# A four-layer convolution chain on one core: storing the Haar coefficients so that a step of the mixing stage reads one contiguous run of DRAM

## The chip, the core and the metric

The kernel runs on one core of a Trainium2 chip. The metric is the device time of one execution in microseconds. Before the change it is 2869.11 us, the median of 7 runs (2862.92 to 2873.05).

## The reference

The input x has shape (4, 64, 256, 256): images, channels, rows, columns, in float32. Four layers follow each other.

```python
x = conv(x, L0)      # per channel: a causal 2-D convolution with an outer-product filter, plus x * bias
x = haar_layer(x)    # L1
x = conv(x, L2)
x = conv(x, L3)

def haar_layer(x):
    f1 = haar2d(x)
    acc = 0
    for i in range(2):
        f4 = einsum('bchw,oc->bohw', f1 * v[i], conv_w[i])
        acc += sign(f4) * relu(abs(f4) - tau[i])
    return haar2d(acc, inverse=True) + x
```

The filters of the convolution layers come from small sine networks. Since the filter of a channel is an outer product, the convolution is a multiplication by one triangular Toeplitz matrix along the rows and another along the columns. The convolutions and the Haar transforms act on one channel at a time; the mixing in L1 acts on all 64 channels at one position. That is why the data changes its order twice, through DRAM.

## The kernel before

The four images are two groups of two. Three phases work on each group.

- **Phase A** (`phase_a`, L422) goes through a group in 32 rounds of two channels. A round loads x (L136, 1 MB), multiplies by the Toeplitz matrices `tx` and `ty` (L149, six DMAs of 64 KB), does the forward Haar transform along one axis on POOL (L355, L357) and along the other on PE (L319), and stores its 1 MB of coefficients in the DRAM tile `coef` of the group (`store`, L481 to L483).
- **Phase B** (`phase_b`, L524) goes through a group in 64 steps. A step takes a 1/64 part of the coefficients of all 64 channels. `load` (L539) fetches it in two DMAs (`ft<-coef`, L545), and also `v` and `tau` for the step (L551, 512 KB each). Per step there are two units: PE mixes the channels (L590), DVE multiplies by v (L605), ACT takes sign and magnitude (L609, L613), DVE subtracts tau and thresholds (L616, L619), POOL adds up (L631 to L635). `store` (L638 to L640) writes the result to the DRAM tile `mixed` in two DMAs.
- **Phase C** (`phase_c`, L687) goes through a group in 32 rounds again: `load` (L694 to L699) fetches a round's 1 MB from `mixed` into the tile `g`, the inverse Haar transform follows, then the two convolutions L2 and L3 (L307), and the output is stored (L766, L762).

The work is laid side by side by a function `beside` (L817), which mixes the pieces of two phases in program order. First comes phase A of group 0 alone, then phase A of group 1 beside phase B of group 0, then a short changeover, then phase C of group 0 beside phase B of group 1, then phase C of group 1 alone. The order on every engine's queue is that order of the program. All DMAs are issued by SP, one after the other, from one queue; a DMA that must wait holds up every DMA behind it.

A DRAM tile for coefficients (`coefficients`, L103) has the shape [2, 32, PAIR]: 64 blocks, each of PAIR elements (L77). Before the change PAIR is 133,120 elements, that is 520 KB. Two functions say which bytes a DMA touches:

- `all_rows` (L415), used by L483 and L699, gives the rows of one round. SBUF partition p = 2m + q belongs to block m. For each q there is one DMA of 64 rows: 8 KB at an offset of (32 q + r) x 8 KB in block m, for round r. So the 64 rows of a DMA lie at a pitch of 520 KB.
- `step_of` (L532), used by L545 and L640, gives the rows of one step. For each channel parity e there is one DMA of 64 rows of 4 KB. They all lie in block 32 e + s // 2, at a pitch of 8 KB; an even step s takes the first half of each 8 KB, an odd step the second half.

Of the kernel before, what the change touches and what calls it, by code (L numbers as in the profile page):

```python
# [47 lines left out]
P = 128  # L48
# [17 lines left out]
NB = B // GROUPS  # L66
CI = 4 // NB
M = CI * NB

ROUNDS = C // CI  # L70
STEPS = C
# [2 lines left out]
C_PIECES = 4 * BLOCKS + 2  # L74
W = 2 * N

PAIR = 2 * ROUNDS * 2 * NB * W + 2 * NB * W  # L77


IMAGES = (GROUPS, NB, ROUNDS, CI, BLOCKS, ROW, N)  # L80
# [11 lines left out]
def conv_haar_kernel(  # L92
# [10 lines left out]
    def coefficients(name):  # L103
        return dram.tile([CI, STEPS // 2, PAIR], F32, tag=name, name=name)

# [308 lines left out]

    def all_rows(grp_tile, r, images):  # L415

        by_q = images.rearrange("(m q) n k -> q m (n k)", q=2)
        n = 2 * NB * W
        at = [grp_tile.offset + (q * ROUNDS + r) * n for q in range(2)]
        return [(bass.AP(grp_tile.tensor, at[q], [[PAIR, P // 2], [1, n]]), by_q[q]) for q in range(2)]  # L420

    def phase_a():  # L422

# [57 lines left out]
        def store(t):  # L481
            for to, f in all_rows(coef[t // ROUNDS], t % ROUNDS, st[t]["f"]):
                nc.sync.dma_start(to, f)  # L483
            st[t].clear()
# [39 lines left out]
    def phase_b(grp):  # L524
# [7 lines left out]
        def step_of(ap, s, images):  # L532

            n = NB * W
            by_e = images.rearrange("(m e) b w -> e m (b w)", e=CI)
            at = [ap.offset + (e * STEPS // 2 + s // 2) * PAIR + s % 2 * n for e in range(CI)]
            return [(bass.AP(ap.tensor, at[e], [[2 * n, P // CI], [1, n]]), by_e[e]) for e in range(CI)]

        def load(s):  # L539
            if s >= STEPS:  # L540
                return
            d = st[s]
            d["f"] = bp.tile([P, NB, W], F32, tag="ft", name=f"ft_{grp}_{s}", bufs=4)
            for rows, f in step_of(coef[grp], s, d["f"]):
                nc.sync.dma_start(f, rows)  # L545
            for name, src in (("v", v), ("tau", taus)):
                t = d[name] = bp.tile([P, 2, W], F32, tag=name, name=f"{name}_{grp}_{s}", bufs=3)

                at = src.offset + s * 4 * W * COPIES
                flat = bass.AP(src.tensor, at, [[2 * W, 2 * COPIES], [0, C // COPIES], [1, 2 * W]])  # L550
                nc.sync.dma_start(t.rearrange("p e w -> p (e w)"), flat)  # L551
# [86 lines left out]
        def store(s):  # L638
            for to, g in step_of(mixed[grp], s, st[s]["g"]):
                nc.sync.dma_start(to, g)  # L640
            st[s].clear()
# [45 lines left out]
    def phase_c():  # L687
# [6 lines left out]
        def load(t):  # L694
            if t >= total:
                return
            st[t]["g"] = big("in", f"g_{t}", 3)
            for rows, g in all_rows(mixed[t // ROUNDS], t % ROUNDS, st[t]["g"]):
                nc.sync.dma_start(g, rows)  # L699
# [263 lines left out]
```

## Time and profile before

| What | Value |
|---|---|
| Median of 7 runs | 2869.11 us |
| The profiled execution itself | 2869.66 us |
| Its span, first to last instruction | 2867.9 us |
| Mean granted TensorE clock | 0.934 |
| PE / PEld busy share | 85% / 68% |
| DVE / ACT / POOL busy share | 55% / 50% / 68% |
| DMA bytes, mean rate | 636.27 MB, 222 GB/s |
| DMAs issued by SP for coef, g | 128 and 128, 512 KB each |
| DMAs issued by SP for ft, mixed | 256 and 256, 256 KB each |

The profile is of one execution. Busy time is that of an engine in all; it says little about what limits a stage, since the stages differ. The times of the stages in this execution, from the first and last issue of their DMAs: the first ft is issued at 452.4 us, the last coef of group 1 at 1264.9 us, the last mixed of group 1 at 2156.9 us. A line such as "ft<-coef SPq ... x256, 256.0 KB, 8.4" gives a kind of DMA, the number of issues, the size of one and the median time from its issue to its landing. The chain of waits is followed back from the last instruction, at each step to what released it.

### The profile page before, as it was taken

What the parts mean: (1) busy time and instruction counts of PE and PEld (TensorE: products, weight loads), DVE (VectorE), ACT (ScalarE), POOL (GpSimd) and SP (SyncE); (2) the same over time, 40 slices, a digit from 0 to 9 for tenths busy, and PEclk for the clock granted to TensorE, in tenths of its full rate; (3) what the DMA queues carried; (4) which work ended last, traced back from release to release, by engine and by line L of the source; (5) the groups of instructions that cost most, each with busy time, mean ns of one, the idle gap of its engine ahead of it and who ended that gap; (6) DMA issues with size and microseconds to landing.
All of it is one profiled execution on the core that took longest, in us unless ns stands there. A gap on an engine that the chain in (4) does not pass through costs nothing.

```text
span 2867.9 us, 119602 instructions
## 1 busy us (share of the span) xinstructions
PE 2437.6 (85%) x53276; PEld 1948.4 (68%) x53276; DVE 1582.9 (55%) x1779; ACT 1428.4 (50%) x2361; POOL 1950.5 (68%) x2422
## 2 busy tenths in 40 slices
PE   6999998677767667759888888898898999999999
PEld 5777776454445444537777666676677888888888
DVE  2453335677777767536777766766772333333333
ACT  1222224566566666527676666676673333333332
POOL 2777876877778777748878767777775555555551
PEclk9999998788888887979999999999999999999999
DMA  5668777799898999766888888888885444444432
GB/s 156 230 211 252 249 270 237 239 274 284 284 286 274 271 282 272 243 194 205 251 266 233 260 249 246 246 261 243 249 253 172 147 141 152 138 157 132 161 114 93
DMA packets 223290, 636.27 MB, mean 222 GB/s; under 512 B 39078, under 2 KB 121671, under 8 KB 190264
## 3 DMA queue, kind: packets, MB, share of 16 engines
q1 hardware_dynamic: 222776, 628.62, 70.5%
q8 instruction: 419, 6.86, 1.0%
q14 instruction: 95, 0.78, 0.1%
HBM read 413.12 MB, written 215.35 MB: 219 GB/s over the span
## 4 chain that ended last, share of the span: by engine, by line
PE 40%; DMA 23%; DVE 8%; POOL 5%; issue 4%; ACT 4%; SPq 3%; DVEq 0%; ACTq 0%; POOLq 0%
PE c1c L307 9%; PE c2r L307 8%; DMA ft<-coef 8%; PE c2c L307 7%; PE c1r L307 6%; DMA v<-in_v 5%; PE c0ps L319 3%; PE f L590 3%; DMA mixed<-gt 2%; DMA tau<-taus 2%; DMA g<-mixed 2%; DVE a L616 2%; DVE x L605 2%; DMA tx<-filt 1%; PE a1ps L307 1%
## 5 line engine op out<-in xcount | busy, mean ns | idle before, releaser
L392 POOL TENSOR_TENSOR i<-i,g 128x16 f32<-128x16 f32 x744 | 394.8, 551 | 477.7 <-ACT g L375 458.7
L590 PE MATMUL f<-ft,mix 64*64 64x512 f32 x2048 | 345.3, 686 | 248.3 <-DMA ft<-coef 173.0
L605 DVE TENSOR_TENSOR x<-f,v 128x1024 f32<-128x1024 f32 x256 | 312.1, 1219 | 261.1 <-PE f L590 129.1
L307 PEld LDWEIGHTS a1ps<-tx,x 64*64 64x64 f32 x8192 | 324.8, 142 | 111.3 <-issue 51.9
L609 ACT ACTIVATE m<-x 128x1024 f32<-128x1024 f32 x256 | 272.2, 1063 | 223.1 <-DVE x L605 165.5
L307 PEld LDWEIGHTS c1c<-ty,ch 64*64 64x64 f32 x8192 | 307.8, 134 | 107.7 <-ACT ch L740 58.3
L307 PE MATMUL a1ps<-tx,x 64*64 64x192 f32 (+3 forms) x8192 | 356.3, 315 | 27.5 <-issue 7.5
L307 PE MATMUL c1c<-ty,ch 64*64 64x256 f32 (+3 forms) x8192 | 341.9, 302 | 34.4 <-issue 24.0
L307 PEld LDWEIGHTS c2r<-tx,cy 64*64 64x64 f32 x8192 | 305.7, 135 | 96.2 <-ACT ch L740 55.5
L307 PEld LDWEIGHTS a2ps<-ty,ay 64*64 64x64 f32 x8192 | 315.8, 142 | 77.5 <-issue 52.4
L307 PE MATMUL a2ps<-ty,ay 64*64 64x256 f32 (+3 forms) x8192 | 346.5, 314 | 14.4 <-issue 10.2
L307 PE MATMUL c2r<-tx,cy 64*64 64x256 f32 (+3 forms) x8192 | 339.3, 303 | 19.8 <-issue 11.7
L616 DVE TENSOR_TENSOR a<-a,tau 128x1024 f32<-128x1024 f32 x256 | 313.8, 1226 | 65.8 <-ACT a L613 64.9
L613 ACT ACTIVATE a<-x 128x1024 f32<-128x1024 f32 x256 | 264.7, 1034 | 168.6 <-DVE m L619 168.4
L631 POOL TENSOR_TENSOR gt<-gt,m 128x1024 f32<-128x1024 f32 x128 | 303.2, 2369 | 58.3 <-DVE m L619 55.7
L307 PE MATMUL c2c<-ty,ch 64*64 64x128 f32 (+3 forms) x8192 | 323.8, 300 | 12.5 <-issue 12.4
L740 ACT COPY ch<-c1r 128x512 f32<-128x512 f32 x256 | 137.2, 588 | 391.5 <-PE c1r L307 391.2
L307 PE MATMUL c1r<-tx,z 64*64 64x64 f32 (+3 forms) x8192 | 325.9, 301 | 5.7 <-issue 5.7
L307 PEld LDWEIGHTS c2c<-ty,ch 64*64 64x64 f32 x8192 | 307.5, 135 | 33.4 <-issue 20.8
L307 PEld LDWEIGHTS c1r<-tx,z 64*64 64x64 f32 x8192 | 304.1, 135 | 36.1 <-issue 21.2
L466 DVE SCALAR_TENSOR_TENSOR x<-x,bias_sb,a2ps 128x512 f32<-128x512 f32 x256 | 179.5, 742 | 269.1 <-PE a2ps L307 247.4
L619 DVE SCALAR_TENSOR_TENSOR m<-a,m 128x1024 f32<-128x1024 f32 x256 | 313.0, 1223 | 22.0 <-DVE a L616 0.5
(71 smaller groups left out, 3200.3 us busy)
## 6 DMA issues: line engine op xcount, KB each, us to landing
coef<-f SPq DMA_DIRECT2D x128, 512.0 KB, 5.7
ft<-coef SPq DMA_DIRECT2D x256, 256.0 KB, 8.4
v<-in_v SPq DMA_DIRECT2D x128, 512.0 KB, 8.4
tau<-taus SPq DMA_DIRECT2D x128, 512.0 KB, 10.2
mixed<-gt SPq DMA_DIRECT2D x256, 256.0 KB, 8.4
g<-mixed SPq DMA_DIRECT2D x128, 512.0 KB, 7.9
x<-in_x SPq DMA_DIRECT2D x63, 1024.0 KB, 6.5
out<-o SPq DMA_DIRECT2D x63, 1024.0 KB, 5.1
```

The source lines that it names most:

```text
L307: nc.tensor.matmul(ps[r][half(c), j % 2, k * ROW :], data[half(r), c, k, bass.ts(j, ROW)], t(r, c)[:, : N - k * ROW], start=k == 0, stop=k ...
L319: nc.tensor.matmul(ps[r][half(c)].rearrange("p h k -> p (h k)"), matrix[half(r)], pairs(r, c).rearrange("p h k -> p (h k)"), start=True, s ...
L392: engine.tensor_tensor(to, s, d, op)
L466: nc.vector.scalar_tensor_tensor(to, old, bias_sb[:, c : c + 1], ps, ALU.mult, ALU.add)
L590: nc.tensor.matmul(un[u]["f4"][half(q), b, :], mixers[0][half(r), bass.ts(i, C)], st[s]["f"][half(r), b], start=True, stop=True, tile_posi ...
L605: nc.vector.tensor_tensor(un[u]["x"], un[u]["f4"], both(u, "v"), ALU.mult)
L609: nc.scalar.activation(un[u]["m"], un[u]["x"], AF.Sign)
L613: nc.scalar.activation(un[u]["a"], un[u]["x"], AF.Abs)
L616: nc.vector.tensor_tensor(un[u]["a"], un[u]["a"], both(u, "tau"), ALU.subtract)
L619: nc.vector.scalar_tensor_tensor(un[u]["m"], un[u]["a"], 0.0, un[u]["m"], ALU.max, ALU.mult)
L631: nc.gpsimd.tensor_tensor(st[s]["g"], st[s]["g"], m, ALU.add)
L740: later(lambda y=y, ps=ps: nc.scalar.copy(y, ps))
```

## The change

Only addresses change. A block keeps its 512 KB of data (2 values of q, 32 rounds, 2 halves, 4 KB each). Inside a block the half h of a row's 8 KB now comes first in the order of addresses, before q and the round. A round's rows are therefore cut into 4 KB pieces, and the rows of one step and one parity lie next to each other, 64 x 4 KB in one run of 256 KB. The padding behind a block shrinks from 8 KB to 4 KB, which makes the pitch 516 KB. `all_rows` returns four pairs of DRAM rows and SBUF rows instead of two, so the loops at L482 and L698 issue four DMAs of 256 KB per round instead of two of 512 KB. `step_of` still returns two.

```diff
-PAIR = 2 * ROUNDS * 2 * NB * W + 2 * NB * W
+PAIR = 2 * 2 * ROUNDS * NB * W + NB * W
...
     def all_rows(grp_tile, r, images):
 
-        by_q = images.rearrange("(m q) n k -> q m (n k)", q=2)
-        n = 2 * NB * W
-        at = [grp_tile.offset + (q * ROUNDS + r) * n for q in range(2)]
-        return [(bass.AP(grp_tile.tensor, at[q], [[PAIR, P // 2], [1, n]]), by_q[q]) for q in range(2)]
+        parts = images.rearrange("(m q) (h n) k -> h q m (n k)", q=2, h=2)
+        n = NB * W
+        pairs = []
+        for h in range(2):
+            for q in range(2):
+                at = grp_tile.offset + ((h * 2 + q) * ROUNDS + r) * n
+                pairs.append((bass.AP(grp_tile.tensor, at, [[PAIR, P // 2], [1, n]]), parts[h][q]))
+        return pairs
...
             n = NB * W
             by_e = images.rearrange("(m e) b w -> e m (b w)", e=CI)
-            at = [ap.offset + (e * STEPS // 2 + s // 2) * PAIR + s % 2 * n for e in range(CI)]
-            return [(bass.AP(ap.tensor, at[e], [[2 * n, P // CI], [1, n]]), by_e[e]) for e in range(CI)]
+            at = [ap.offset + (e * STEPS // 2 + s // 2) * PAIR + s % 2 * P // CI * n for e in range(CI)]
+            return [(bass.AP(ap.tensor, at[e], [[n, P // CI], [1, n]]), by_e[e]) for e in range(CI)]
```

## The prediction

> **What bounds the kernel now.** I read the page's forty slices first, then a table of stretches, then the chain of waits stage by stage, then the DMA issues, and last SP's own order of issue.
>
> ```profile
> PE   6999998677767667759888888898898999999999
> ...
> DMA  5668777799898999766888888888885444444432
> ```
>
> Read the two rows together. The front (to about 450 us) and the back (from about 2160 us) are full on PE and easy on DMA. Between 450 and 1200 us the DMA row stands at 8 and 9 while PE falls to 6 and 7. The stretches (us, then busy PE, PEld, DVE, ACT, POOL, then clock, DMA share, GB/s) say it in numbers:
>
> ```profile
> 200.00:300.00 100.00, 95.46 (x2242) 77.65 (x2235) 35.88 (x53) 27.25 (x49) 76.65 (x130) 0.98 0.80 249
> ...
> 600.00:750.00 150.00, 107.61 (x1768) 71.04 (x1768) 108.72 (x101) 95.22 (x130) 118.64 (x136) 0.85 0.92 283
> ...
> 1570.00:1720.00 150.00, 126.12 (x2697) 97.99 (x2699) 102.86 (x104) 94.37 (x153) 105.44 (x110) 0.98 0.85 247
> ...
> 2400.00:2640.00 240.00, 239.00 (x6266) 212.39 (x6261) 84.07 (x120) 91.05 (x201) 135.83 (x190) 1.00 0.44 145
> ```
>
> So there are four stages: A alone (PE 95%), A with B (DMA 0.92), C with B (both high), C alone (PE over 99%, DMA 0.44). The chain of waits, cut to 450-1200, 1270-2160 and 2160-2867 us, agrees:
>
> ```profile
> by line: DMA ft<-coef 20.1%; DMA v<-in_v 17.4%; DVE a L616 5.6%; DMA x<-in_x 4.6%; issue 4.4%; DVE x L605 4.2%; DVE m L619 3.4%; DVE x L466 3.3%; PE f L590 3.2%; DMA tx<-filt 3.2%; DMA tau<-taus 2.8%; DMA coef<-f 2.8%; DMA mixed<-gt 2.6%; A
> ...
> by line: PE c1c L307 9.8%; issue 8.6%; PE c2r L307 8.3%; DMA ft<-coef 7.9%; PE f L590 7.5%; DMA g<-mixed 6.5%; DMA mixed<-gt 5.7%; DMA tau<-taus 4.8%; PE c2c L307 4.8%; PE c1r L307 4.3%; PE c0ps L319 3.2%; SPq L149 2.7%; DVE o L759 2.3%; DV
> ...
> by line: PE c2r L307 23.7%; PE c1c L307 22.5%; PE c2c L307 21.6%; PE c1r L307 20.4%; PE c0ps L319 9.5%; issue 0.9%; DMA g<-mixed 0.7%; DVEq L958 0.2%; ACT ch L740 0.2%; ACTq L958 0.1%; ACT g L375 0.0%; DVE o L759 0.0%; ACTq L375 0.0%
> ```
>
> Adding the DMA entries: about 0.54 of the first stretch is transfer time on the chain, about 0.28 of the second (20.1 + 17.4 + 4.6 + 3.2 + 2.8 + 2.8 + 2.6, and 7.9 + 6.5 + 5.7 + 4.8 plus some smaller ones that the full chain gives), under 0.01 of the third. Those shares are my exchange rate from DMA time to kernel time. The transfers concerned are these (KB each, median us to landing):
>
> ```profile
> coef<-f SPq DMA_DIRECT2D x128, 512.0 KB, 5.7
> ft<-coef SPq DMA_DIRECT2D x256, 256.0 KB, 8.4
> ...
> mixed<-gt SPq DMA_DIRECT2D x256, 256.0 KB, 8.4
> g<-mixed SPq DMA_DIRECT2D x128, 512.0 KB, 7.9
> ```
>
> Last, SP's place on the chain. A piece of the chain in time order (start, us, what):
>
> ```profile
> 704.26 0.75 SPq L483
> 705.01 0.05 issue
> 705.06 0.02 SPq L545
> 705.08 0.03 issue
> 705.10 0.71 SPq L545
> 705.82 0.05 issue
> 705.87 9.46 DMA ft<-coef
> ```
>
> Here ft, which PE will need, is issued only after the coef stores of L483, because one in-order queue issues both. SP's timeline gives the price of an issue:
>
> ```profile
> 104.37 0.52 SPq L149 DMA_DIRECT2D ty<-filt  x1
> 105.73 1.14 SPq L483 DMA_DIRECT2D coef<-f  x2
> ```
>
> 1.14 us for two, so about 0.57 us each, and g, ft and mixed issues have medians near that.
>
> **What the Trainium skill says.** The page "DMA: Bandwidth & Descriptors", section "Latency and other measured facts", reports that rows at a pitch of large powers of two lose up to half the rate, that 4 KB of padding restores it, and that contiguous rows are fine too. The old pitch of 520 KB and the new one of 516 KB are both padded, and the 8 KB pitch of a step is not in its table. The trace shows the padded layout running well: data packets of 8 KB take 309 ns at the fast end and coef lands in 5.7 us. Its section "Why a DMA increments its semaphore by 16 and not by 1" derives the engine count from the slowest dimension; 64 rows use 16 engines before and after. The trace agrees: 38,567 four-byte completion packets for 2,413 DMAs, 16 each. Its section "Rules for kernel authors" wants few large transfers; here the trace has its own durations, which I use.
>
> **The change, part by part.** The order of issue on every engine stays; PE, DVE, ACT and POOL keep the same instructions. On SP only L483 and L699 change, from two DMAs of 64 rows x 8 KB to four of 64 rows x 4 KB. Bytes are equal.
>
> 1. *Packets of coef and g.* The trace's packets by size: 4 KB take 159 ns at the fast end (5th percentile), 225 in the mean; 8 KB take 309 and 364. Two for one costs 2 x 159 - 309 = 9 ns at best, 2 x 225 - 364 = 86 ns at worst. Each DMA is 4 rows per engine. Of the 128 coef DMAs, 54 fall in A with B: 216 rows per engine, 2 to 19 us of DMA time, times 0.54: 1 to 10. Of the 128 g DMAs, 58 fall in C with B: 232 rows, 2 to 20 us, times 0.28: 1 to 6. I take 3 us for both, near the low end, because coef already runs at the fast end. The 64 coef DMAs before 450 us and the 62 g DMAs after 2160 us are hidden under PE; without that cover they would cost as much again.
>
> 2. *256 more issues on SP.* At 0.57 plus 0.1 us between issues, 54 more between 450 and 1200 us are 36 us of SP time, 58 more in C with B 39 us. Most of it replaces waiting: SP stands waiting for earlier landings anyway (the waits of SP list 33.2 us of L149 for v, 28.0 for tau, and a dozen rows more in the first stage). Summing the chain's own pieces, L483 lies on it for 16.9 us and L699 for 2.9, so at most another 20 us, at least 0. Queued behind them on SP are mixed, ft, v and tau of the next step, and PE (L590) and DVE (L605) wait for those. This includes the three joints where a whole group must land before the next stage starts (448, 1265 and 2160 us), where two more issues stand in the open, about 1.2 us each. I take 8 us. In A alone the 58 more issues (39 us over 350) are hidden by PE at 95%; if A were not PE-bound they would show.
>
> 3. *The window of landings.* The trace's DMAs use eight landing semaphores in turn (100 to 105, 107, 108), and SP waits for the DMA eight issues back. With coef or g in the window, eight DMAs hold less than before, but still 2 MB (8 x 256 KB), some 7 us of work at 283 GB/s; I count 0, between minus 5 and plus 5 us, as the places of the waits shift by two.
>
> 4. *A step's rows become one run of 256 KB (ft, mixed).* The trace has no such 4 KB transfer. Nearest rows: x is contiguous, and yet it has one of the longest pieces of the chain in A with B (13.32 us, at 1124.68); v and tau come from contiguous 64 KB, each row read eight times, and land in 8.4 and 10.2 us. Bound from above: if all 512 packets per engine of ft and as many of mixed fell from 225 to 159 ns, 1024 x 66 ns = 68 us of DMA time per stage, 68 x (0.54 + 0.28) = 55 us gained. Bound from below: ft becomes as slow against today as tau stands against ft (10.2 to 8.4, a fifth): 45 ns on 225, 512 x 45 = 23 us of DMA time per stage, times 0.82: 19 us lost. I take 0: being contiguous shows no advantage in this trace, and both ends stay for the range.
>
> Sum: 3 + 8 = 11 us. On the profiled execution of 2869.66 us (span 2867.9, 1.8 outside it) that is 2880.7; the median of the runs is 0.55 lower, so I say 2880 us. Every wait stays in its place, and what is late next is ft after L483, as now.
>
> **Rivals.** *R1, contiguous rows are faster (the other side).* One mechanism: ft and mixed reach fewer memory channels at 4 KB of every 8 KB, and the new layout spreads them. Place: the two B stages. Price: half the bound, 27 us, less the 11 us of cost: 2854. It decides from the point where a fifth of the bound (11 of 55 us, 13 of the 66 ns a packet) is won. For it: ft is the largest entry of the chain. Against: the neighbours that are contiguous, x, v and tau, show no such advantage. *R2, contiguity hurts and SP shows fully.* 19 us from point 4, 20 from SP, 4 from the packets: 43, so 2912. For it: one queue issues everything and L483 stands right ahead of ft. Against: SP spends much of its time in waits. *R3, nothing shows:* SP's issues replace waits altogether and the packets cost 2: 2871; it is the low end of my own case.
>
> **How the numbers follow.** The measurement can tell about 0.2%, 5.7 us. My case, with its own range 2868 to 2896, gets 0.52, of which R3's corner and its surroundings within 0.2% are 0.17; R1 0.28 (2815 to 2866), of which 0.02 is within 0.2%; R2 0.20 (2896 to 2925). Faster 0.26, same 0.19, slower 0.55. Leaving a tenth or so off each end gives 2842 to 2904.
>
> **What would show it.** Right: SP has 256 issues each of coef and g; the DMA share between 600 and 750 us stays at 0.92 or above with the same GB/s; ft and mixed land in about 8.4 us; L483 on the chain nearly doubles; C alone is unchanged. R1: ft and mixed land clearly sooner, GB/s there rises above 283 and the wait of PE L590 for ft shrinks from 142.1 us. R2: ft lands later and the waits of L590 and L605 grow. Wrong altogether: a change in A alone or C alone of more than 5 us, where I count everything as hidden.

## The result

The changed kernel takes 2841.67 us (median of 13 runs, 2824.6 to 2852.46). The kernel before, run beside it, takes 2866.35 us (median of 34 runs, 2854.89 to 2885.23). The ratio is 0.9909, with a 95% interval of 0.989 to 0.9928: faster by 0.9%, about 26 us. The forecast was 2880 us, slower by 11 us; the direction was wrong, and the low end of the range of 2842 to 2904 us misses the median by a hair.

The profiled execution of the changed kernel took 2837.24 us, with a span of 2835.5 us. The stretches that were shown of the kernel before, now of the kernel after (us; busy PE, PEld, DVE, ACT, POOL; clock, DMA share, GB/s):

```profile
200.00:300.00 100.00, 95.71 (x2313) 79.89 (x2305) 34.46 (x50) 27.80 (x51) 81.04 (x142) 1.00 0.84 250
600.00:750.00 150.00, 105.44 (x1668) 67.49 (x1672) 108.87 (x103) 91.61 (x122) 111.66 (x120) 0.83 0.92 275
1570.00:1720.00 150.00, 131.96 (x2824) 102.70 (x2820) 106.71 (x108) 99.70 (x160) 109.77 (x113) 0.97 0.85 259
2400.00:2640.00 240.00, 239.23 (x6290) 212.40 (x6282) 82.65 (x118) 92.35 (x204) 134.63 (x192) 1.00 0.46 148
```

The DMA share is the same as before in the stretches of A beside B and C beside B. The rate rose from 247 to 259 GB/s in the third row and fell from 283 to 275 in the second, so short stretches don't tell the story. The DMA issues do show a change (KB each, median us to landing):

```profile
coef<-f SPq DMA_DIRECT2D x256, 256.0 KB, 4.8
ft<-coef SPq DMA_DIRECT2D x256, 256.0 KB, 6.5
...
mixed<-gt SPq DMA_DIRECT2D x256, 256.0 KB, 7.3
g<-mixed SPq DMA_DIRECT2D x256, 256.0 KB, 6.3
```

ft lands in 6.5 us where it took 8.4, mixed in 7.3 instead of 8.4. That looks like the proof of faster reads, but the first experiment below takes it away again. The chain between 450 and 1200 us in the kernel after:

```profile
by line: DMA v<-in_v 18.7%; DMA tau<-taus 13.3%; DMA ft<-coef 12.2%; DMA x<-in_x 7.9%; DVE x L610 5.3%; DVE a L621 4.9%; DMA mixed<-gt 3.8%; issue 3.4%; DVE m L624 3.3%; POOL f L357 3.0%; POOL fw L355 3.0%; DVE x L471 2.9%; PE f L595 2.5%; 
```

ft has gone from 20.1% to 12.2%, but v and tau together have grown by more, from 20.2% to 32.0%. The whole chain has 672 us of DMA before and 669 us after: what has changed is which of a step's loads lands last.

The four stages, cut at the first issue of ft, the last of coef and the last of mixed, are better places to look. Before: A alone 452.4, A beside B 812.5, C beside B 892.0, C alone 711.0 us. After: 446.1, 806.5, 878.6, 704.2. These are single executions, and the profiled run of a kernel lies up to 13 us from the kernel's median, so a stage's difference of 6 us is weak evidence by itself. The two middle stages of the kernel before (those of the kernel after stand with experiment 6):

```profile
452.40:1264.90 812.50, 576.60 (x9389) 383.65 (x9385) 557.43 (x555) 470.60 (x648) 614.74 (x712) 0.84 0.85 263
1264.90:2156.90 892.00, 764.12 (x16468) 617.79 (x16463) 615.88 (x633) 581.74 (x934) 652.41 (x668) 0.95 0.83 245
```

Below, *busy DMA time* is the summed time of the packets in the kernel's own DMA queue, divided by 16 engines, counted from the trace of a stage. The DMA share in the views also holds two small queues that fetch instructions, and is about 0.01 higher than busy DMA time over the length of the stage.

### The profile page after: what moved, and what is told of

Its sections match the earlier page's. It is cut to its first block, busy times and chain, and to the rows that moved or that the text cites. A ratio compares the mean times of both kernels' runs of the same rounds, so it can differ in the third digit from the quotient of the medians.

```text
span 2835.5 us, 120133 instructions
## 1 busy us (share of the span) xinstructions
PE 2434.7 (86%) x53276; PEld 1942.1 (68%) x53276; DVE 1583.4 (56%) x1779; ACT 1428.6 (50%) x2361; POOL 1951.8 (69%) x2422
## 4 chain that ended last, share of the span: by engine, by line
PE 38%; DMA 24%; DVE 10%; POOL 5%; ACT 4%; issue 4%; SPq 2%; DVEq 0%; ACTq 0%; POOLq 0%
PE c1c L307 9%; PE c2r L307 8%; DMA v<-in_v 7%; PE c2c L307 7%; PE c1r L307 6%; DMA ft<-coef 5%; DMA tau<-taus 5%; PE c0ps L319 3%; PE f L595 3%; DVE x L610 3%; DVE a L621 2%; DMA x<-in_x 2%; DVE m L624 2%; DMA mixed<-gt 1%; DMA g<-mixed 1%
## 5 line engine op out<-in xcount | busy, mean ns | idle before, releaser
L307 PE MATMUL a1ps<-tx,x 64*64 64x256 f32 (+3 forms) x8192 | 359.3, 317 | 24.1 <-ACT f L484 6.8
L307 PE MATMUL c1c<-ty,ch 64*64 64x128 f32 (+3 forms) x8192 | 339.2, 301 | 21.4 <-issue 11.0
L307 PE MATMUL c1r<-tx,z 64*64 64x128 f32 (+3 forms) x8192 | 329.3, 302 | 6.0 <-issue 6.0
L307 PE MATMUL c2c<-ty,ch 64*64 64x256 f32 (+3 forms) x8192 | 320.4, 297 | 6.4 <-issue 6.3
```

The source lines that it names most:

```text
L307: nc.tensor.matmul(ps[r][half(c), j % 2, k * ROW :], data[half(r), c, k, bass.ts(j, ROW)], t(r, c)[:, : N - k * ROW], start=k == 0, stop=k ...
```

## The experiments

Three theories were put up. *Layout*: the addresses of a step's rows give the gain. *Pieces*: issuing 256-KB instead of 512-KB DMAs for coef and g gives it. *Pitch*: 516 KB instead of 520 KB gives it. All ratios are against the kernel before on the same chip, with 95% intervals.

**1. The pieces alone.** The old addresses, but four DMAs:

```diff
-        by_q = images.rearrange("(m q) n k -> q m (n k)", q=2)
...
+        parts = images.rearrange("(m q) (h n) k -> h q m (n k)", q=2, h=2)
...
+                at = grp_tile.offset + ((q * ROUNDS + r) * 2 + h) * n
+                pairs.append((bass.AP(grp_tile.tensor, at, [[PAIR, P // 2], [1, n]]), parts[h][q]))
```

> The layout of before (8 KB per round and row at 520 KB, step rows 4 KB at a pitch of 8 KB), but a round's stores and loads issued as four DMAs of 64 rows x 4 KB, as in the change. Layout theory (contiguous step rows give the gain): 1.000 to 1.005 of before, because only the issues and the smaller packets are left. Pieces theory (256-KB DMAs land sooner, the window of eight landings turns faster): 0.991, the whole gain of the change. If both have a share, about 0.995.

Measured: 0.9989 (0.9975 to 1.0003). The 256 further issues and the smaller packets together cost nothing that shows, and they aren't the gain. Yet ft in this kernel:

```profile
ft<-coef SPq DMA_DIRECT2D x256, 256.0 KB, 6.1
...
mixed<-gt SPq DMA_DIRECT2D x256, 256.0 KB, 7.6
```

6.1 us for ft, even less than after the change, with none of its gain. So a shorter time to landing is no sign of a shorter kernel here. The likely reason, which no run separates: that time counts what is queued ahead, and with halved DMAs of coef and g a queue of the same number of DMAs holds fewer bytes.

**2. The addresses alone.** The layout of the change, with two DMAs per round, each of 64 rows x 2 pieces of 4 KB:

```diff
+            rows = [[PAIR, P // 2], [2 * ROUNDS * n, 2], [1, n]]
+            pairs.append((bass.AP(grp_tile.tensor, at, rows), parts[q]))
```

> The layout of the change (step rows contiguous, 516 KB pitch, packets of 4 KB), but a round's stores and loads issued as two DMAs of 64 rows x 2 pieces of 4 KB, 512 KB each, as many issues as before. Layout theory: 0.991 or a little below (SP saves 256 issues). Pieces theory: 1.000 to 1.003.

Measured: 0.9924 (0.9906 to 0.9942). The layout carries the gain. The difference of 0.0015 to the full change isn't resolved.

**3. The pitch alone.**

```diff
-PAIR = 2 * ROUNDS * 2 * NB * W + 2 * NB * W
+PAIR = 2 * ROUNDS * 2 * NB * W + NB * W
```

> The kernel before with one constant changed: the padding behind a block is 4 KB instead of 8 KB, so the pitch of a round's rows is 516 KB instead of 520 KB. Layout theory and pieces theory: 1.000. Pitch theory (516 KB spreads a round's rows better than 520 KB, and the rest of the change costs nothing): 0.991.

Measured: 0.9998 (0.9982 to 1.0014). The pitch theory falls. This kernel issues the same DMAs as the kernel before and is as fast, so its trace tells how far two traces differ without a cause:

```profile
450.20:1259.90 809.70, 569.86 (x9360) 381.04 (x9355) 555.95 (x553) 471.18 (x648) 613.10 (x708) 0.85 0.87 264
1259.90:2152.30 892.40, 766.12 (x16485) 619.69 (x16479) 615.89 (x634) 582.23 (x935) 652.30 (x669) 0.95 0.83 245
```

Busy DMA time in the two stages together is 1429.9 us here and 1416.9 us in the trace before.

**4. Holes of 4 KB.** The change with a factor GAP on every address within a block; here GAP is 2, so a step's rows are again 8 KB apart:

```diff
-            return [(bass.AP(ap.tensor, at[e], [[n, P // CI], [1, n]]), by_e[e]) for e in range(CI)]
+            return [(bass.AP(ap.tensor, at[e], [[GAP * n, P // CI], [1, n]]), by_e[e]) for e in range(CI)]
```

> The change with holes: the same DMAs, the same 4-KB pieces, but a step's rows of 4 KB lie at a pitch of 8 KB with 4 KB unused between them, and a block takes 1028 KB. Layout theory (the step's 4-KB rows must be dense): 1.000 to 1.005 of before, the gain is lost. Pieces theory: 0.991, the gain stays.

Measured: 1.0024 (1.001 to 1.0038). Same DMAs and packets as in the change; the gain is gone. Nor is it that the rows of two neighbouring steps interleave, for here they don't. What is left is the pitch of a step's rows, or that of the blocks, which the holes moved too (experiment 7). If it is the rows, two readings remain. Either they must be dense, or 8 KB is a bad pitch.

**5. Holes of 8 KB.** The same edit with GAP = 3.

> The change with larger holes: a step's rows of 4 KB at a pitch of 12 KB, 8 KB unused between them, a block takes 1540 KB. Spread theory (at 4 KB of every 8 KB a step's rows reach only half of the memory's channels, an odd multiple of 4 KB reaches all): 0.991 of before, the gain is back. Density theory (rows must follow each other without a hole): 1.002 as with the pitch of 8 KB, or slower.

Measured: 0.9896 (0.987 to 0.9922). The gain is back, with two thirds of the memory between the rows unused. Density theory falls. "Adjacent" in the name of the change isn't what matters.

**6. Holes of 12 KB.** GAP = 4.

> The change with a step's rows of 4 KB at a pitch of 16 KB, 12 KB unused between them; a block takes 2052 KB. Spread theory (the pitch's power of two decides which share of the channels a step's rows reach: 4 and 12 KB all, 8 KB a half, 16 KB a quarter): slower than the 8-KB pitch with the same DMAs (1.002), 1.01 to 1.03 of before. If only touching rows or a small hole mattered: 0.990 to 1.002.

Measured: 1.0215 (1.0183 to 1.0247). As the kernels stand, 4 and 12 KB are fast, 8 KB is slow and 16 KB slowest. That is the order of the spread theory, but the blocks lie 2052 KB apart here, and experiment 8 takes most of the 16-KB loss away from the rows. Stages 2 and 3 (A beside B, C beside B) of the runs, each in its own fence, the pitch of a step's rows ahead of it. 4 KB, the change:

```profile
446.10:1252.60 806.50, 577.53 (x9373) 380.72 (x9368) 557.54 (x554) 468.86 (x645) 614.20 (x711) 0.85 0.87 265
1252.60:2131.20 878.60, 765.50 (x16538) 616.36 (x16534) 617.79 (x634) 583.63 (x938) 655.05 (x672) 0.96 0.83 249
```

12 KB:

```profile
445.60:1249.60 804.00, 572.10 (x9372) 381.01 (x9368) 556.83 (x554) 469.65 (x645) 613.80 (x712) 0.85 0.87 266
1249.60:2138.60 889.00, 766.92 (x16521) 618.52 (x16516) 617.33 (x634) 583.38 (x938) 654.95 (x672) 0.95 0.84 246
```

8 KB, the kernel of experiment 4:

```profile
453.80:1274.00 820.20, 572.27 (x9327) 380.32 (x9323) 556.09 (x553) 468.71 (x645) 611.01 (x705) 0.83 0.87 261
1274.00:2175.40 901.40, 771.13 (x16540) 617.57 (x16536) 617.13 (x634) 583.15 (x938) 654.54 (x672) 0.95 0.84 242
```

16 KB:

```profile
451.50:1310.60 859.10, 590.78 (x9376) 381.71 (x9372) 557.00 (x554) 469.08 (x645) 612.86 (x713) 0.82 0.88 249
1310.60:2214.60 904.00, 773.06 (x16509) 622.34 (x16505) 618.13 (x634) 583.04 (x938) 654.13 (x671) 0.95 0.84 242
```

Read the first number after each stretch and the DMA share near the end together. Stage 2 lasts from 804 to 859 us while the DMA share stays at 0.87 or 0.88. In other words the stage's length follows the time that the DMA engines are busy: from the change to the 16-KB kernel the stage grows by a factor of 859.1 / 806.5 = 1.065, and busy DMA time goes from 697.7 to 747.5 us, 1.07. DVE, ACT and POOL do the same work in the same busy time.

**7 and 8. The pitch between blocks.** The holes also moved the blocks apart (1028, 1540, 2052 KB). These two runs keep the rows dense and move the blocks:

```diff
-PAIR = 2 * 2 * ROUNDS * NB * W + NB * W
+PAIR = 2 * 2 * 2 * ROUNDS * NB * W + NB * W
```

and the same with 4 in the place of the first 2.

> The change with one constant changed: blocks lie at a pitch of 1028 KB instead of 516 KB; a step's rows stay dense. If the loss with step rows at 8 KB (1.002 against 0.991) came from the step's rows: 0.991 here. If it came from the pitch between blocks, which was 1028 KB there too: 1.002.

> The change with one constant changed: blocks at a pitch of 2052 KB, a step's rows dense. If the loss with step rows at 16 KB (1.0215) came from the step's rows alone: 0.991. If the slower loads of g in phase C alone (23 us of that stage) came from the pitch of 2052 KB: 0.999 or a little above, with A beside B as fast as in the change and C alone slow. If all came from the pitch: 1.02.

Measured: 0.9922 (0.9896 to 0.9947) and 1.011 (1.0086 to 1.0134). Stages 2 and 3 at 1028 KB, then at 2052 KB:

```profile
450.30:1259.50 809.20, 575.06 (x9420) 380.85 (x9416) 558.16 (x555) 471.26 (x648) 615.40 (x715) 0.85 0.87 265
1259.50:2152.30 892.80, 761.27 (x16467) 612.44 (x16463) 616.41 (x634) 582.26 (x936) 652.95 (x669) 0.95 0.83 245
```

```profile
450.10:1289.00 838.90, 579.03 (x9348) 376.05 (x9344) 556.55 (x554) 470.14 (x645) 612.80 (x710) 0.84 0.88 255
1289.00:2174.30 885.30, 769.55 (x16524) 620.82 (x16518) 617.64 (x634) 583.55 (x938) 655.05 (x671) 0.95 0.84 247
```

At 1028 KB nothing is lost, so the loss in experiment 4 came from the step's rows: with the blocks at the same pitch, rows at 8 KB cost 0.0102 (1.0024 against 0.9922). The transfers are slower there: a packet of 4 KB takes 217 ns in the mean of stage 2 and 226 in stage 3, against 214 and 221 with dense rows.

At 2052 KB the pitch between blocks costs about 0.020 against the change by itself. So of the 0.031 that the 16-KB run lies above the change about two thirds is the blocks' and, if the two losses add up, only 0.0105 the step's. That is no more than rows at 8 KB cost, within an uncertainty of about 0.004. The expectation of experiment 6, 1.01 to 1.03, was met largely through the blocks, which the spread theory didn't speak of, and its further loss from 8 to 16 KB isn't shown. (Single traces do show more: busy DMA time of the two stages rises from 1431.9 to 1451.7 us for the 8-KB rows and from 1459.3 to 1499.1 us for the 16-KB rows. But the traced run of the 16-KB kernel lies 13 us above its median, and that of the 2052-KB kernel 11 us below.)

1.011 fits none of the three expectations for 2052 KB. The stage of C alone, first after the change, then with 2052 KB:

```profile
2131.20:2835.50 704.30, 690.22 (x18100) 614.01 (x18089) 238.22 (x340) 259.11 (x568) 366.24 (x513) 0.99 0.44 143
```

```profile
2174.30:2891.60 717.30, 692.72 (x18110) 616.26 (x18102) 238.33 (x340) 259.20 (x568) 366.12 (x513) 0.99 0.48 140
```

Here g is the only user of that pitch. The mean of the 4-KB packets in this stage goes from 173 to 232 ns, and the DMA share from 0.44 to 0.48 at fewer bytes per time. The stores of coef in A alone don't mind: 164 and 168 ns. Yet in C beside B, with the same loads of g, the mean of all 4-KB packets is about the same (220 against 219 ns). A beside B was expected to stay fast at 2052 KB; it took 838.9 us instead of 806.5, which I can't assign to one of its transfers. Why a pitch of 2052 KB is slow stays open.

**9 and 10. Loads or stores.** The change for one of the two DRAM tiles:

```diff
+        if all(grp_tile is not d for d in dense):
+            by_q = images.rearrange("(m q) n k -> q m (n k)", q=2)
...
+            return [(bass.AP(grp_tile.tensor, at[q], [[WIDE, P // 2], [1, n]]), by_q[q]) for q in range(2)]
```

> The change for coef alone (stores of phase A in four DMAs, ft read from contiguous runs); mixed keeps the layout, the pitch and the two DMAs of before. Read theory (it is the loads of ft that get faster): 0.991 to 0.993. Write theory (it is the stores of mixed): 0.999 to 1.000. Both share: 0.995.

> The change for mixed alone (stores of a step into contiguous runs, g in four DMAs); coef keeps the layout, the pitch and the two DMAs of before. Read theory: 0.998 to 1.000. Write theory: 0.991 to 0.993. Both share: 0.995.

Measured: 0.9955 (0.9937 to 0.9973) for coef, 0.9969 (0.9952 to 0.9985) for mixed. Both share: the loads of ft have a part in the gain, and the stores of mixed have one. The two gains add up to 0.0076 of 0.0091. The stores of coef and the loads of g were cut into pieces along with them, which experiment 1 has as costing nothing.

**11 to 14. Fewer issues for a step.** The first asks for SP's share, and is the version that beats both kernels. One DMA takes both parities of a step:

```diff
+            at = ap.offset + s // 2 * PAIR + s % 2 * P // CI * n
+            rows = [[n, P // CI], [STEPS // 2 * PAIR, CI], [1, n]]
+            return [(bass.AP(ap.tensor, at, rows), images.rearrange("p b w -> p (b w)"))]
```

> The layout of the change, but ft and mixed are issued as one DMA of 512 KB (128 rows of 4 KB, both parities) instead of two of 256 KB; SP issues 256 DMAs fewer. If SP's issue time is on the path (the term of my sum, 0 to 20 us for 256 issues): 0.984 to 0.990 of before. If smaller DMAs help by turning the window of landings faster: 0.992 to 0.996. No effect: 0.991.

Measured: 0.9791 (0.9768 to 0.9815), 2817.15 us in the median, faster than any of the three expectations. The stages 2 and 3:

```profile
451.40:1234.60 783.20, 572.72 (x9429) 381.91 (x9424) 557.52 (x555) 469.55 (x648) 615.64 (x715) 0.85 0.90 274
1234.60:2106.30 871.70, 760.58 (x16466) 614.24 (x16459) 617.70 (x634) 580.95 (x935) 652.69 (x669) 0.96 0.85 250
```

Here the other factor moves: the DMA share rises from 0.87 to 0.90, at a busy DMA time of 698.7 us in stage 2, as in the change. The transfers are no faster; the engines stand idle less.

The same edit in the old layout, a split by halves of the partitions, and coef and g in wide DMAs too:

> The kernel before with one edit: ft and mixed are issued as one DMA of 512 KB per step (both parities) instead of two of 256 KB; addresses, pitch and packets are those of before. If the gain of one DMA per step (1.2% on top of the change) is independent of the layout: 0.987 to 0.989 of before. If it needs the fast layout: 0.995 to 1.000.

> The layout of the change, ft and mixed again in two DMAs of 256 KB per step, but split by halves of the partitions (0 to 63 and 64 to 127, both parities in each) instead of by parity. If the one-DMA version gained by its number of issues (SP's time, or bytes in the window of eight landings): 0.991, as the change. If it gained by its row order over the partitions: 0.979.

> The one-DMA version with coef and g too in DMAs of 128 rows x 4 KB (two of 512 KB per round instead of four of 256 KB); SP issues 512 DMAs fewer than in the change's count for these four tensors. If fewer, larger DMAs keep helping: 0.972 to 0.977 of before. If it is only the step's DMAs that count: 0.979 to 0.981.

Measured: 0.9948 (0.9931 to 0.9964), 1.0108 (1.0076 to 1.0141), 0.9816 (0.9784 to 0.9848). The old layout gains 0.5% from it, less than expected for an independent gain; the fast layout gains 1.2%. Both expectations missed for the halves: as many DMAs as in the change, and 2% slower than it. The edit moves two things at once: each DMA touches 64 neighbouring partitions instead of every second one of all 128, and its rows are 32 from each of two blocks instead of 64 from one. The one-DMA version reads from two blocks as well and isn't slow, which speaks for the partitions, but no run separates the two. The DMA share of stage 2 there:

```profile
446.50:1274.10 827.60, 620.64 (x9444) 407.40 (x9440) 557.34 (x556) 470.86 (x648) 615.91 (x717) 0.85 0.92 259
```

The engines are busier (0.92) and move less (259 GB/s); a packet of 4 KB takes 234 ns in the mean instead of 213. Wide DMAs for coef and g take another 256 issues from SP and add nothing. So what counts is the step's DMAs. Why is open: SP's time, the bytes that eight landings can cover, or which partitions and blocks a DMA touches. One DMA instead of two changes all three, and the halves show that the last can cost 2% at the same number of DMAs and bytes.

## Why the prediction was wrong

- **Step 4 failed: "I take 0: being contiguous shows no advantage in this trace."** The new layout was worth 0.8% (0.9909 against 0.9989 with the same DMAs at the old addresses), some 23 us. I compared ft with other transfers that are contiguous, x, v and tau, and asked whether being contiguous helps. The trace before had no row with another pitch than 8 KB for the same transfer, and the neighbours differ in packet size and repetition. From a comparison that couldn't show an advantage I concluded that there was none. The question was another one: is 8 KB a bad pitch? A 12-KB pitch, not contiguous at all, is as fast (0.9896).
- **R1 came near by luck.** R1 named a mechanism, 4 KB of every 8 KB reaching only a part of the memory, and gave it 27 us with a chance of 0.28; the gain was 23 us. But it got there by two errors that cancel. It took half the bound, 33 ns off each of the 2048 packets per engine of ft and mixed, 68 us of DMA time. Three pairs of traces show 20 to 26 us less in the two stages: the pieces alone and the change (1444.7 and 1418.5), rows at 8 KB and dense rows with blocks at 1028 KB (1451.7 and 1431.9), rows at 8 and at 12 KB (1451.7 and 1427.8). That is an estimated 10 to 13 ns a packet, about a fifth of the bound, and a rough figure, since two traces without a cause differ by 13 us (experiment 3). The exchange rate, 0.41 on average, was too low by about the same factor. The 11 us of cost that R1 also carried weren't there. That a pitch of 8 KB is slow is shown; that memory channels are the reason is argued, and rows at 16 KB, which should then be slower still, aren't shown to be.
- **The exchange rate was wrong.** I multiplied DMA time by the chain's share of transfers, 0.54 and 0.28. In the twelve kernels that move a step in two DMAs by parity, busy DMA time is 0.860 to 0.870 of the length of stage 2 (0.844 in the trace before alone), and 0.819 to 0.831 of stage 3. From the 12-KB to the 16-KB kernel, stage 2 has 53 us more busy DMA time and lasts 55 us longer. So a microsecond of DMA time costs about one of kernel time in stage 2, and the steady share of stage 3 points the same way. Why isn't shown; my reading is that the chain switches between DMA, DVE and PE within a step, while all of it waits on the same filled queue.
- **Step 1, packets of coef and g: the size was off, and it didn't matter.** I took 3 us on the path, out of 4 to 39 us of DMA time. The split leaves 1444.7 us of busy DMA time in the two stages, 15 us more than the kernel of experiment 3 and 28 more than the trace before, and yet the kernel stayed at 0.9989. Where that time went isn't shown. The count also left out the 10 coef and 8 g DMAs between 1200 and 1270 us, which changes little. The trace before is the odd one, with a share of 0.844 in stage 2 where experiment 3, the same DMAs and as fast, has 0.860. This is why busy time before and after (1416.9 and 1418.5) seems to say that nothing happened.
- **Step 2, SP's issues: 8 us expected, none measured.** The pieces alone, with all 256 further issues, stayed at 0.9989, and the new layout with as many issues as before is no faster than the change (0.9924 against 0.9909). L483 did not double on the chain; its successor L488 lies on it for 5.3 us after, against 16.9. The low bound of 0 held; that the issues fell into waits is the likely reading. Issues of the step's own DMAs are another matter (experiment 11).
- **Step 3, the window of landings**, counted at 0 for coef and g: nothing here speaks against it. For ft and mixed the window may count, as the one-DMA version leaves open.
- **Right:** SP issues 256 each of coef and g; the order of everything stays; the DMA share between 600 and 750 us stays at 0.92, though at 275 GB/s instead of 283. The wait of PE for ft between 450 and 1200 us, which R1 expected to shrink, didn't (142.1 to 140.1 us).
- **A sign of "wrong altogether" came as well:** A alone is 6.3 us shorter and C alone 6.8 us, where I had put 5 us as the limit. A alone lasts 445.6 to 453.8 us over all the traces, so that may be chance. C alone is not: it lasts 703.1 to 706.7 us in the eight kernels that load g in four DMAs at block pitches under 2052 KB, and 709.4 to 711.6 us in the five that load it in two of 64 rows. I had those loads as hidden. What in the stage gets shorter is open.

## What to carry to other kernels

For rows of a few KB in DRAM, try another pitch, and don't ask only whether they are adjacent: here 4 and 12 KB are fast, and 8 KB costs about 1% of the kernel. Vary one pitch at a time, since rows and the blocks that hold them move together: most of the loss at 16 KB was the blocks'. Where a stage's DMA share stays the same from version to version, price a change in busy DMA time over that share, not by the chain; then ask separately what raises the share. And compare a transfer only with the same transfer at another address, and by the time of the kernel: its time to landing fell from 8.4 to 6.1 us without any gain.

## What the runs showed of the hardware that was not expected

- The pitch matters at 8 KB for DMAs of 64 rows x 4 KB on 16 engines: 1.0024 against 0.9922 for dense rows with the same block pitch, and against 0.9896 at 12 KB. The Trainium skill, "DMA: Bandwidth & Descriptors", section "Latency and other measured facts", lists pitches from 512 KiB up, with a clear loss from 2 MiB on (164 GB/s against a full 214).
- The same section has 4 KB of padding restore the full rate at a pitch of 4 MiB, for rows of 16 KiB. With 4 KB of padding on 2 MB, the 4-KB packets of C alone, where g is loaded, took 232 ns instead of 173 at 516 KB, while in A alone, where coef is stored, they took 168 instead of 164. The measurement decides here: for these loads in that stage a padded pitch of 2052 KB is still slow. No run has 2 MB without padding beside it.
- Two DMAs of 64 neighbouring partitions each are slower than two of every second partition: 1.0108 against 0.9909, at the same sizes and count. The blocks that their rows come from differ as well, so the partitions are the likely cause, not a shown one.
